# Unread products of the identity in TensorE's planned pauses, in a fused attention and recurrence kernel

## The chip, the cores and the metric

The kernel runs on one core of a Trainium2 chip. The metric is the device time of one execution in microseconds (us). The engines are TensorE (PE in the profile; its weight loads are PEld), VectorE (DVE), ScalarE (ACT), GpSimd (POOL) and SyncE (SP), which only issues transfers. "Granted clock" is the share of TensorE's full clock that its throttle lets through, as the profile records it.

## The reference, cut to what matters

Two layers follow each other on `x` of shape (16, 112, 512), all in float32. The first is a cross attention with 16 heads of width 32 over a normalised context of (16, 375, 512). The second is one block of a recurrent network: a data-dependent mix of each token with the one before it, five projections, a state of 16 x 16 per head (32 heads) that decays and takes in an outer product at each of the 112 steps, a normalisation over each head, a gate, and a feed-forward part.

```python
a = layer_norm(ctx)                         # attention
Q, K, V = x @ Wq.T, a @ Wk.T, a @ Wv.T      # per head
x = x + tanh(gate) * (softmax(Q K^T * scale) V) @ Wo.T

xa = ln(x); sx = shift(xa) - xa             # recurrence
xk, xw, xv, xr, xg = xa + sx * (maa + tanh-mix(xa, sx))
w = exp(-exp(time_decay + tanh(xw @ td_w1) @ td_w2))
def step(s, r, k, v, w):                    # 112 times
    return k v^T + w * s,  r . (u * k v^T + s)
x1 = x + group_norm(out) * silu(xg @ Wg.T) @ Wo.T
y = x1 + sigmoid(xr2 @ Wfr.T) * (relu(xk2 @ Wfk.T)**2 @ Wfv.T)
```

## The kernel before

**A recorder and a planner.** The program isn't written out in the order in which it runs. `planned` (line 599) calls the same operations on a `Recorder`, which only notes them. Generators for the parts (`attention`, and for each of eight groups of two batches `front`, `begin`, `middle` and `back`) note their operations with a place in an ideal order. A `Planner` (line 384) then plays through a model of the engines. Neighbouring TensorE products of one output are joined to a unit, every other operation is a unit of its own. `choose` takes the unit that can start first, with the place as a tie-break, and `commit` (line 532) books it: it gives each new tile a slot, asks a model of the array (`Array.run`, line 357) how long the products take, and notes when results and slots become free. `emit` (line 571) writes the instructions in exactly the planned order, with no reordering behind it, so that each engine's queue is the plan's order for that engine. The waits between engines come from the tiles that instructions share: who touches a tile waits for those before it in the plan's order that touched it in a way that conflicts.

**The model of TensorE.** For a full product of n columns `Array.run` counts `2 * (n * 2 / 2.4 + 2)` ns; for a transpose it takes the larger of a streaming term, `0.868` ns per column of the weights, and 109 ns. `Array.start` puts the start of a unit at the time when its inputs are ready or when the array is done, whichever is later. What lies between the array's end and that start is a pause in the plan. The plan knows nothing of the clock throttle.

**PSUM.** The eight banks of 512 float32 columns are seven slots of the tag `ps_bank`, which all products share in turn, and one of `ps_w`. `ps_w` holds the decays w of one chunk of channels: `decays_up` (line 1261) has VectorE clear its first columns and ScalarE write the rest with two exponentials, and `scans` (line 1301) has VectorE read it in two scans for each of the four steps of the chunk. It has 448 columns in use.

**The recurrence.** `middle` (line 1348) runs 16 steps n for each group. A step loads the values from DRAM, spread over partitions (`chk_kv`), multiplies them by the keys on VectorE and GpSimd, scans (VectorE, into `chk_st`, which has three slots), multiplies by r (GpSimd), and is summed by TensorE two steps later (`summed`, line 1321) with narrow products into one accumulator for each chunk. So a slot of `chk_st` is free again once TensorE has summed it. After the last step `back` follows: `norm_and_gate`, the projection `wo1`, a layer norm (its two sums are products with the constant `mean_w`), and the projections `wfk`, `wfr` and `wfv`.

**The tail.** Attention of later groups fills TensorE while a group's recurrence keeps VectorE and GpSimd busy. For the last two groups less and less of it is left.

## Time and profile before

| | us |
|---|---|
| median of 3 runs | 1387.72 (1385.05 to 1392.49) |
| the profiled execution, own time | 1388.27 |
| its span | 1386.5 |
| its mean granted TensorE clock | 0.963 |
| VectorE busy | 922.6 |
| GpSimd busy | 663.7 |
| ScalarE busy | 593.9 |

In the profile's rows an operation is named by its helper line (L596, the line of `emit` that calls all of them), so the names of the tiles tell groups apart: output tile, arrow, input tiles, with buffer numbers left out. A group's row has the number of instructions, the busy time and the mean duration of one, and then the idle time of the engine just before them with what ended it. A float32 product shows as two matmul records, each with a weight load of its own, and a transpose as one. The duration of a matmul record includes its way through the array; records overlap, so the pace of a row of products is read from the distance of their starts. A timeline row is start, duration of the merged piece, engine, operation, count, and in brackets the idle time before it. A row by stretches of time is the stretch, its length, busy time and records, the granted clock, and the share and rate of the DMA.

### The profile page before, as it was taken

How to read it: one execution, taken by the hardware profiler on the slowest of the kernel's cores; microseconds unless marked ns; L12 is line 12 of the kernel's file. 1: busy time of each engine (PE TensorE's matmuls, PEld its weight loads, DVE VectorE, ACT ScalarE, POOL GpSimd, SP SyncE). 2: the span in 40 equal slices, each digit the busy share in tenths (PEclk: the TensorE clock that was granted, in tenths of full speed). 3: DMA queues.
4: the chain of work that ended last, by engine and by line, in shares of the span. 5: the costliest groups of instructions: out<-in, count | busy, mean ns of one | idle time of the engine just before them, and what ended most of it. 6: DMA issues, size and time to landing. Idle time of an engine off the chain costs nothing.

```text
span 1386.5 us, 23595 instructions
## 1 busy us (share of the span) xinstructions
PE 1292.1 (93%) x8484; PEld 961.8 (69%) x8484; DVE 922.6 (67%) x1743; ACT 593.9 (43%) x1476; POOL 663.7 (48%) x644
## 2 busy tenths in 40 slices
PE   8999999989999999989999999989999898888867
PEld 5656577566966688566976589656985686767636
DVE  4345548975488664985577844994569669857942
ACT  2444624464245533664235631665325624233312
POOL 3001126843466442953546524771458357735750
PEclk9999999999999999999999999999999999979859
DMA  9401137321764057521774038521464155608621
GB/s 314 138 24 51 29 83 231 88 68 58 245 183 109 32 150 228 129 70 53 207 215 115 17 103 259 149 74 53 144 216 114 47 164 162 185 25 231 182 59 44
DMA packets 119990, 175.00 MB, mean 126 GB/s; under 512 B 14320, under 2 KB 92016, under 8 KB 119616
## 3 DMA queue, kind: packets, MB, share of 16 engines
q1 hardware_dynamic: 119232, 172.85, 42.9%
q8 instruction: 67, 1.10, 0.3%
q10 hardware_dynamic: 576, 0.52, 0.1%
q14 instruction: 51, 0.42, 0.1%
q0 software_dynamic: 64, 0.10, 0.0%
HBM read 164.52 MB, written 8.91 MB: 125 GB/s over the span
## 4 chain that ended last, share of the span: by engine, by line
PE 68%; DVE 13%; DMA 6%; ACT 5%; issue 4%; POOL 3%; SPq 1%; DVEq 0%; ACTq 0%; POOLq 0%
PE ps_bank L596 68%; DVE chk_st L596 5%; DMA chk_kv<-dram_vd 3%; ACT hp_pr L596 2%; DVE hp_pr L596 2%; DVE chk_kv L596 2%; POOL chk_st L596 1%; SPq L596 1%; DVE big_xa L596 1%; DMA ctxp_ctx<-in_ctx 1%; DMA slabs_slab<-in_wq 1%; ACT big_xa L596 1%; DMA slabs_slab<-in_wg 1%; ACT tmp_tmp L596 1%; DVE sm_st L596 0%
## 5 line engine op out<-in xcount | busy, mean ns | idle before, releaser
L596 POOL TENSOR_TENSOR chk_st<-chk_st,chk_r 128x448 f32<-128x448 f32 x256 | 316.2, 1257 | 137.1 <-DVE chk_st L596 133.5
L596 DVE TENSOR_TENSOR_SCAN chk_st<-ps_w_w,chk_kv 128x448 f32<-128x448 f32 x256 | 263.7, 1069 | 7.1 <-POOL chk_kv L596 4.6
L596 POOL TENSOR_TENSOR chk_kv<-chk_kv,chk_k 128x444 f32<-128x444 f32 x128 | 155.4, 1216 | 142.1 <-DMA chk_kv<-dram_vd 141.7
L596 PE MATMUL ps_bank<-big_x,slabs_slab 128*128 128x224 f32 x1024 | 205.0, 356 | 3.2 <-DMA slabs_slab<-in_wg 1.8
L596 PEld LDWEIGHTS ps_bank<-big_x,slabs_slab 128*128 128x128 f32 x1024 | 195.0, 192 | 10.6 <-issue 4.4
L596 PE MATMUL ps_bank<-ctxp_aT,keep_wk 128*128 128x375 f32 x512 | 174.2, 487 | 2.5 <-ACT hp_prT L596 2.0
L596 PE MATMUL ps_bank<-keep_wv,ctxp_aT 128*125 128x512 f32 x384 | 169.2, 592 | 0.0
L596 ACT ACTIVATE hp_pr<-hp_pr,sm_mn 112x375 f32<-112x375 f32 x256 | 152.9, 599 | 34.6 <-DVE sm_mn L596 34.1
L596 DVE TENSOR_TENSOR chk_kv<-chk_kv,chk_k 128x444 f32<-128x444 f32 x128 | 127.0, 995 | 45.9 <-DMA chk_kv<-dram_vd 45.7
L596 DVE CUSTOM_DVE_ANT_0 hp_pr<-ps_bank,hp_mb 112x375 f32<-112x375 f32 x256 | 124.8, 539 | 37.6 <-PE ps_bank L596 35.9
L596 PEld LDWEIGHTS ps_bank<-ctxp_aT,keep_wk 128*128 128x128 f32 x512 | 94.5, 191 | 65.2 <-ACT hp_prT L596 3.2
L596 PEld LDWEIGHTS ps_bank<-keep_wv,ctxp_aT 128*125 128x125 f32 x384 | 71.7, 188 | 84.0 <-issue 81.7
L596 PE MATMUL ps_bank<-chk_st,keep_td1c 128*32 128x224 f32 x1024 | 81.8, 375 | 33.2 <-POOL chk_st L596 28.5
L596 PE MATMUL ps_bank<-keep_ident,hp_pr 112*125 112x112 f32 x768 | 104.7, 281 | 8.6 <-ACT hp_prT L596 4.5
L596 PEld LDWEIGHTS ps_bank<-keep_ident,hp_pr 112*125 112x125 f32 x768 | 90.5, 188 | 31.4 <-ACT hp_prT L596 6.7
L596 POOL TENSOR_TENSOR big_x<-big_x,big_xa 128x448 f32<-128x448 f32 x48 | 59.8, 1260 | 82.2 <-DVE big_x L596 73.0
L596 ACT COPY chk_kv<-chk_s 128x8 f32<-128x8 f32 x112 | 22.5, 201 | 157.5 <-DMA chk_kv<-dram_vd 145.8
L596 PEld LDWEIGHTS ps_bank<-chk_st,keep_td1c 128*32 128x32 f32 x1024 | 29.7, 111 | 74.4 <-POOL chk_st L596 52.4
L596 DVE SCALAR_TENSOR_TENSOR big_x<-ps_bank,keep_vecs,big_sx 128x224 f32<-128x224 f32 x160 | 59.4, 440 | 26.7 <-PE ps_bank L596 26.6
L596 ACT COPY hp_prT<-ps_bank 125x448 f32<-125x448 f32 x112 | 58.2, 525 | 37.8 <-PE ps_bank L596 37.6
L596 ACT COPY kvp_v<-ps_bank 125x512 f32<-125x512 f32 x48 | 27.6, 582 | 99.0 <-PE ps_bank L596 99.0
L596 PE MATMUL ps_bank<-kvp_kT,kvp_qT 32*112 32x375 f32 x512 | 66.0, 519 | 0.2 <-ACT kvp_oR L596 0.2
(130 smaller groups left out, 1998.6 us busy)
## 6 DMA issues: line engine op xcount, KB each, us to landing
chk_kv<-dram_vd SPq DMA_DIRECT2D x512, 111.5 KB
slabs_slab<-in_wo SPq DMA_DIRECT2D x32, 512.0 KB
ctxp_ctx<-in_ctx SPq DMA_DIRECT2D x15, 672.0 KB
slabs_slab<-dram_wv1c SPq DMA_DIRECT2D x16, 512.0 KB
slabs_slab<-in_wk SPq DMA_DIRECT2D x16, 512.0 KB
slabs_slab<-in_wr SPq DMA_DIRECT2D x16, 512.0 KB
slabs_slab<-in_wg SPq DMA_DIRECT2D x16, 512.0 KB
slabs_slab<-in_wfk SPq DMA_DIRECT2D x16, 512.0 KB
```

Source lines behind the costliest of these rows:

```text
L596: call(*[real(a) for a in op.args], **{k: real(v) for k, v in op.kwargs.items()})
```

## The change

Wherever the plan has a pause of TensorE of more than 500 ns in front of a unit, and the unit's planned start lies after 30 us, the changed `emit` first issues products of the 128 x 128 identity with its own first 64 columns. Their number is 80% of (pause - 250 ns), divided by 110 ns and rounded down. Nobody reads the result. It goes to columns 448 to 511 of a bank: that of the unit itself, where the plan found its slot free before the array was done, and that of `ps_w` otherwise. For that the `ps_w` tile gets 512 columns, of which the first 448 are used as before. The planning isn't touched: the planned times don't count the new products, and all other instructions keep their order on every engine.

```diff
 SAME_MODE = 3.0
+PAUSE, FILL, FILLER, WARM, SPARE = 500.0, 0.8, 110.0, 30e3, 64
...
-        self.table = None
+        self.table, self.early = None, None
...
                 tile.slot = self.slot(tile)
+                if unit.engine == "tensor" and tile is unit.ops[0].writes[0].tile:
+                    unit.early = tile.slot.free_at <= self.array.end
...
         if engine == "tensor":
+            unit.pause = start - self.array.end if self.array.mode else 0.0
             ends = self.array.run(unit, start)
...
+    def spare(self, unit):
+        slot = unit.ops[0].writes[0].tile.slot if unit.early else None
+        slot = slot or self.recorder.tags["ps_w", "w"].slots[0]
+        return slot.real[:, 512 - SPARE : 512]
...
+        ident = self.recorder.tags["keep", "ident"].slots[0].real
...
+                if unit.engine == "tensor" and unit.pause > PAUSE and unit.start > WARM:
+                    spare = self.spare(unit)
+                    for _ in range(int((unit.pause - PAUSE / 2) * FILL / FILLER)):
+                        nc.tensor.matmul(spare, ident, ident[:, :SPARE], start=True, stop=True)
...
-            w_ps[c] = ps_w.tile([P, 2 * N], F32, tag="w", name=f"wp_{g}_{c}")
+            w_ps[c] = ps_w.tile([P, 512], F32, tag="w", name=f"wp_{g}_{c}")[:, : 2 * N]
```

In the changed program these are 610 products in 78 batches, the longest of 65. They raise TensorE's products from 4754 to 5364. 39 batches with 293 products write to the bank of `ps_w`, the others to a slot of `ps_bank`.

## The prediction

> **What bounds the kernel now.** I read the page's busy shares first, then the granted clock in its slices, then the chain that ended last.

> ```profile
> PE 1292.1 (93%) x8484; PEld 961.8 (69%) x8484; DVE 922.6 (67%) x1743; ACT 593.9 (43%) x1476; POOL 663.7 (48%) x644
> ```
> ```profile
> PEclk9999999999999999999999999999999999979859
> ```
> ```profile
> PE 68%; DVE 13%; DMA 6%; ACT 5%; issue 4%; POOL 3%; SPq 1%; DVEq 0%; ACTq 0%; POOLq 0%
> ```

> TensorE is busy 93% of the span and is 68% of the chain, so what delays it mostly delays the end. Its clock is full for most of 35 slices and drops in the last eight. The clock by stretches (us, PE busy and records, granted clock, DMA) shows all that there is to win:

> ```profile
> 297.68:301.09 3.41, 3.41 (x20) 0.50 0.85 225
> ...
> 1096.39:1103.22 6.83, 5.73 (x36) 0.50 0.00 0
> ...
> 1277.30:1290.96 13.66, 8.28 (x31) 0.50 0.38 90
> 1318.26:1348.99 30.73, 17.73 (x57) 0.50 0.16 44
> ...
> sum 102.43, PE 77.44; mean PE 5.96
> ```

> The thirteen throttled stretches last 102.4 us at clock 0.50, with 77.4 us of TensorE work in them. At full clock that work takes half, so the **gain is at most 38.7 us**: 6.7 before 1085 us, 9.0 from there to 1210, 6.8 in 1210 to 1240, 4.1 at 1277, 12.1 after 1310. Part of it is waiting for others and can't be won.

> **The price of one product.** The change adds 610 products in 78 batches, by the built program's order; nothing else moves on any engine, only waits are added. Every fp32 product is two records here, each with its own weight load (3730 products twice and 1024 transposes once make the 8484 of both rows); four products in a row with the same weights (mean_w of the late layer norms) still have eight loads, so an unchanged identity will be loaded again too. A pass streams 64 columns: 224 columns take 0.189 us in dense stretches (53 records in 10 us), so 0.054 us a pass and 0.108 a product, which is the planner's FILLER. But the weights are 128 columns wide. Two rows price their load (start, duration, what, count):

> ```profile
> 1313.46 0.30 PEld L596 LDWEIGHTS ps_bank<-tmp_tmp,keep_td1c 128*128 128x128 f32 x2 [0.82 <-ACT tmp_tmp L596]
> ```
> ```profile
> 332.42 1.39 PEld L596 LDWEIGHTS ps_bank<-keep_ident,hp_pr 112*125 112x125 f32 x12
> ```

> One load lasts 0.19 us, and two end after 0.30, so the second begins 0.11 after the first. Twelve transposes, whose matmuls stream less than the loads take, run at (1.39 - 0.19) / 11 = 0.109 us each. I take **0.109 us a pass, 0.218 a product**, twice what the planner thinks: 610 make 133 us. The ends are 0.108 (load hidden) and 2 x (0.19 + 0.054) = 0.49 (nothing overlaps); the value lies with the two rows that show loads back to back.

> [...]

> **Where the batches stand.** They fill 80% of a *planned* pause at half their real price; the trace has the real pauses. I laid each batch beside the gap of the trace in front of its product (start of that matmul less the end of streaming before it, less 0.15 us for the ordinary hand-over). "Excess" adds up what each batch takes beyond its own gap. "Carried" lets all idle time of TensorE in the stretch absorb lateness, and is what is left at its end.

> | us | batches, products | us at 0.218 | excess | carried |
> |---|---|---|---|---|
> | to 1085 | 47, 170 | 37.1 | 19.5 | 5.7 |
> | 1085 to 1200 | 9, 92 | 20.1 | 11.1 | 4.3 |
> | 1200 to 1240 | 8, 86 | 18.7 | 16.2 | 10.1 |
> | 1240 to 1310 | 4, 54 | 11.8 | 7.7 | 4.2 |
> | after 1310 | 10, 208 | 45.3 | 34.3 | 24.4 |

> In one ledger over the whole span the excess is 89 us and the carried lateness 46. 31 batches with 170 products stand before gaps under 0.2 us: the planner expected a pause that the chip doesn't have.

> A wait is added as well. 39 batches (293 products) write the last columns of the decay bank ps_w, which VectorE's scans read and ScalarE fills; they wait for the last such instruction before them in the plan's order, and later ones wait for them. Behind a waiting batch stand all of TensorE's products.

> **Stretch by stretch**, lateness against clock won:

> - To 1085 us: most of it is one long TensorE chain, with VectorE chains of 20 to 40 us between, where lateness is caught up. Midway between 5.7 and 19.5: +12. The eight-product batches in the 2.1 us pauses before 296, 614 and 935 fit, and lift windows like 294.27 to 297.68 (PE busy 1.55 us, then half clock) well above that. All 6.7 won: **+5.3**.
> - 1085 to 1200: batches of 10, 17, 27 and 12 overrun by 2.0, 2.6, 1.7 and 2.0; some is caught up behind DMA of chk_kv at 1174 to 1191. +7.6 less 6.5 of the 9.0: **+1.1**.
> - 1200 to 1240: 34 products wait for a VectorE memset of ps_w that ended at 1218.06, so end at 1225.5, and 1.3 us of summing and filling follows; the products of maa1 began at 1220.77. 31 more follow by 1230. The projection at 1234.44 starts some 7 us late, of which 3 come back by the full clock: **+4.0**.
> - 1240 to 1310: 26 products wait for the scan that ended at 1285.68, end at 1291.4, and the projection of 1288.38 becomes 3.4 late, less 1.2 of clock: **+2.2**.
> - After 1310: the decisive batch. Rows of TensorE, then of VectorE:

> ```profile
> 1322.99 3.14 PE L596 MATMUL ps_bank<-chk_st,keep_td1c 128*32 128x224 f32 x12 [3.26 <-POOL chk_st L596]
> 1326.63 0.96 PE L596 MATMUL ps_bank<-chk_st,keep_td1c 128*32 128x224 f32 x4 [0.50 <-POOL chk_st L596]
> ...
> 1335.09 0.96 PE L596 MATMUL ps_bank<-chk_st,keep_td1c 128*32 128x224 f32 x4 [0.29 <-POOL chk_st L596]
> ```
> ```profile
> 1332.73 1.09 DVE L596 TENSOR_TENSOR_SCAN chk_st<-ps_w_w,chk_kv 128x448 f32<-128x448 f32 x1 [2.39 <-POOL chk_kv L596]
> ```

>   Before the sums of chk_st that now run from 1325.17 on stand 65 products that wait for the *last* scan of the kernel, which ended at 1333.82. That scan is itself late: 12 products wait for the scan of 1316.74 and end at 1319.4, and the decays wait for them; 12 more end at 1324.2 and sums follow for 0.6; 32 then end at 1331.8, before the sum of 1322.99, which frees the slot of the last step's scan; that starts at 1332.6 in place of 1328.27. The last scan so ends at 1338.2, +4.3. Then 65 x 0.218 = 14.2 gives 1352.4, and 1.3 us of sums 1353.7, where they end at 1335.9 now: +17.8. In the closing chain the batches of 7, 31, 4, 15 and 29 add 0.5, 2.1, 0.6, 0.9 and 3.3, and the full clock takes 2.9 from the projection at 1343.27 and 3.1 from the two groups behind it: +1.4. Together **+19.2**.

> Sum: 5.3 + 1.1 + 4.0 + 2.2 + 19.2 = +31.8. The profiled execution took 1388.27 us (span 1386.5 and 1.8 around it), 0.6 over the median of 1387.72, so 1388.3 + 31.8 = **1420 us**, 2.3% slower.

> **What the clock needs** is the other open cost. In the trace a pass of 0.054 us streaming in 0.109 is 49% activity. A window at 331.81 with almost only transposes (45% streaming) kept the clock, and windows under 35% mostly lost it, so the fillers should hold it. At half clock a pass streams 0.107 us, beside 0.109 of load, so the price stays.

> [...]

> **Rivals.**

> 1. *The load of an unchanging weight is hidden* (faster). Then a product costs 0.108, the excess is 36 us and the carried lateness 2; about 12, less some 30 of clock: 1370 us. It decides below about 0.15 us a product, where lateness and gain balance. For it: a load can run beside a matmul. Against: loads never start closer than 0.11 in rows of two. Chance 0.12.
> 2. *Everything absorbs* (no change). The carried 46 less all 38.7: 1396 at most, a little under that where scans are ahead. For it: VectorE's full stretches at 240 to 290. Against: the closing chain has no slack. Chance 0.10.
> 3. *The clock isn't held*, since the identity's products don't count or TensorE stands idle at the new waits: +32 and about 30 not won, 1450; with the price over 0.3 more, over 1480. For it: 65 products wait some 5.7 us with TensorE idle. Chance 0.10.
> 4. The forecast, 1400 to 1457: chance 0.68. Its low end is the carried 46 less most of the clock, its high end the excess of 89 less half of it (1388 + 69).

> **Numbers.** About 0.5% (7 us) is what a measurement of this kernel can tell from no change. Faster 0.12 (rival 1), same 0.09 (most of rival 2), slower 0.79. The range 1393 to 1457 leaves out rival 1 and the upper half of rival 3.

> **What would show it.** In the profile after: 1220 added records of identity matmuls with a load each, starting 0.109 us apart; PEld busy up by over 100 us; the mean granted clock up from 0.963 to about 0.99; the 65 products as one block of 14 us right behind the last scan; new waits of VectorE and ScalarE on TensorE at ps_w; the long TensorE pieces before 1085 little changed. Loads closer than 0.08 us, or a block of 7 us, would make me wrong towards faster; a clock still at 0.5 in the closing 60 us towards slower.

## The result, and the profile after

The changed kernel takes **1460.34 us** (median of 4 runs, 1455.50 to 1462.31) against 1389.41 us (1385.05 to 1392.49) for the kernel before. The ratio is 1.0508, with a 95% interval of 1.0466 to 1.055. It is slower, as forecast, but by 71 us in place of 32, and 3 us above the range. The profiled execution has a span of 1460.3 us.

From the page of the kernel after, the busy shares, the granted clock in 40 slices, and the chain by engine:

```profile
PE 1415.4 (97%) x9704; PEld 1113.2 (76%) x9704; DVE 923.3 (63%) x1743; ACT 593.1 (41%) x1476; POOL 663.9 (45%) x644
```
```profile
PEclk9999999999999999999999999999999997988579
```
```profile
PE 78%; DVE 9%; DMA 5%; issue 3%; ACT 2%; POOL 2%; SPq 1%; DVEq 0%; ACTq 0%; POOLq 0%
```

The 1220 new records are there. VectorE, ScalarE and GpSimd are busy as long as before; only TensorE is busier, by 123 us, and its share of the chain rises from 68% to 78%. The clock row looks almost as it did: the mean granted clock is 0.965 against 0.963. The throttled stretches of the kernel after say more (stretch, length, PE busy and records, granted clock, DMA):

```profile
1200.38:1203.79 3.41, 3.41 (x10) 0.50 0.74 188
1220.86:1241.34 20.48, 20.32 (x96) 0.50 0.00 1
1289.13:1292.54 3.41, 3.41 (x9) 0.50 0.61 196
1306.19:1319.85 13.66, 13.66 (x61) 0.50 0.22 54
1347.15:1408.59 61.44, 54.35 (x277) 0.50 0.07 20
sum 102.40, PE 95.15; mean PE 19.03
```

Before 1200 us nothing is throttled any more (granted clock 1.00 from 30 to 1200 us, 0.99 in the kernel before): there the products do what the change is for. But the sum is 102.4 us again, as in the kernel before. The throttling has moved into the last 260 us, and in its longest stretches TensorE is busy most of the time (88% in the last one). It is busy mainly with the new products. Here is the last stretch, in TensorE's timeline after (start, duration, what, count, idle time before), in two pieces that meet at 1377 us:

```profile
1344.95 3.41 PE L608 MATMUL ps_w_w<-keep_ident 128*128 128x64 f32 x24 [2.31 <-DVE chk_st L611]
...
1350.55 5.35 PE L608 MATMUL ps_w_w<-keep_ident 128*128 128x64 f32 x24 [1.29 <-DVE chk_st L611]
1355.83 0.98 PE L611 MATMUL ps_bank<-chk_st,keep_td1c 128*32 128x224 f32 x8
1356.74 13.92 PE L608 MATMUL ps_bank<-keep_ident 128*128 128x64 f32 x64
1370.59 0.98 PE L611 MATMUL ps_bank<-chk_st,keep_td1c 128*32 128x224 f32 x8
```
```profile
1377.36 27.99 PE L608 MATMUL ps_w_w<-keep_ident 128*128 128x64 f32 x130 [5.80 <-DVE chk_st L611]
1405.29 2.47 PE L611 MATMUL ps_bank<-chk_st,keep_td1c 128*32 128x224 f32 x24
1407.69 2.19 PE L608 MATMUL ps_bank<-keep_ident 128*128 128x64 f32 x14
...
1410.52 7.03 PE L608 MATMUL ps_bank<-keep_ident 128*128 128x64 f32 x62
```

The 65 products (130 records, two to a product) stand behind the last scan, as forecast, and take 27.99 us, 0.215 a pass. The 32 products take 13.92 us, 0.218 a pass. At 1410.52 the clock is full again, and 62 records (31 products) take 7.03 us, 0.113 a pass. So a pass of these products took about twice as long at clock 0.50. VectorE's timeline after shows who waits for the two batches of 12 and 32 (the idle time is in the brackets):

```profile
1355.99 1.09 DVE L611 TENSOR_TENSOR_SCAN chk_st<-ps_w_w,chk_kv 128x448 f32<-128x448 f32 x1 [5.59 <-PE ps_w_w L608]
...
1371.76 2.07 DVE L611 TENSOR_TENSOR_SCAN chk_st<-ps_w_w,chk_kv 128x448 f32<-128x448 f32 x2 [8.63 <-PE ps_bank L611]
```

Both scans stand on the path to the last one. The first waits for the bank that the fillers write, the second for a slot of `chk_st` that the sum at 1370.59, behind the 32 products, sets free.

The same product's start after less its start before gives the lateness along the span (places by the kernel before): 3.7 us at 1197, 18.9 at 1238, 28 at 1311, 43.5 at the last scan (1332.73 before, 1376.22 after), 71.7 where the sums of chk_st end, 73.8 at the end. So 70 of the 74 us arise in the last fifth.

### The profile page after: what moved, and what is told of

Its sections match the earlier page's. It is cut to its first block, busy times and chain, and to the rows that moved or that the text cites. A ratio compares the mean times of both kernels' runs of the same rounds, so it can differ in the third digit from the quotient of the medians.

```text
span 1460.3 us, 26039 instructions
## 1 busy us (share of the span) xinstructions
PE 1415.4 (97%) x9704; PEld 1113.2 (76%) x9704; DVE 923.3 (63%) x1743; ACT 593.1 (41%) x1476; POOL 663.9 (45%) x644
## 4 chain that ended last, share of the span: by engine, by line
PE 78%; DVE 9%; DMA 5%; issue 3%; ACT 2%; POOL 2%; SPq 1%; DVEq 0%; ACTq 0%; POOLq 0%
PE ps_bank L611 67%; PE ps_w_w L608 6%; PE ps_bank L608 5%; DVE chk_st L611 4%; DMA chk_kv<-dram_vd 2%; DVE hp_pr L611 1%; SPq L611 1%; DVE chk_kv L611 1%; DMA ctxp_ctx<-in_ctx 1%; POOL chk_st L611 1%; DMA slabs_slab<-in_wq 1%; ACT hp_pr L611 1%; DMA dram_vd<-chk_v 1%; DMA slabs_slab<-in_wg 1%; ACT big_xa L611 0%
## 5 line engine op out<-in xcount | busy, mean ns | idle before, releaser
L611 DVE TENSOR_TENSOR_SCAN chk_st<-ps_w_w,chk_kv 128x448 f32<-128x448 f32 x256 | 264.1, 1071 | 27.6 <-PE ps_bank L611 8.6
L611 PE MATMUL ps_bank<-big_x,slabs_slab 128*128 128x224 f32 x1024 | 202.0, 353 | 1.7 <-DMA slabs_slab<-in_wg 1.7
L611 PEld LDWEIGHTS ps_bank<-keep_wv,ctxp_aT 128*125 128x125 f32 x384 | 71.7, 187 | 84.1 <-issue 81.0
L608 PE MATMUL ps_w_w<-keep_ident 128*128 128x64 f32 x586 | 100.3, 343 | 18.6 <-DVE chk_st L611 11.5
L608 PEld LDWEIGHTS ps_w_w<-keep_ident 128*128 128x128 f32 x586 | 95.6, 255 | 29.4 <-DVE chk_st L611 14.6
L608 PEld LDWEIGHTS ps_bank<-keep_ident 128*128 128x128 f32 x634 | 81.6, 208 | 8.5 <-issue 6.7
L608 PE MATMUL ps_bank<-keep_ident 128*128 128x64 f32 x634 | 84.9, 292 | 0.0
L611 PE MATMUL ps_bank<-chk_st,keep_td1c 128*32 128x224 f32 x1024 | 69.7, 374 | 3.9 <-DVE sm_mn L611 3.1
```

The source lines that it names most:

```text
L608: nc.tensor.matmul(spare, ident, ident[:, :SPARE], start=True, stop=True)
L611: call(*[real(a) for a in op.args], **{k: real(v) for k, v in op.kwargs.items()})
```

## The experiments

**Theory A** after this result: the long batches make the loss, since they run at half clock, where a pass costs 0.214 us because the weight load is slower too (333 ns in the block of 65, 192 ns in that at 1410.52), and where a stream that fills only half of the pass doesn't bring the clock back (27.99 us at 0.50 in the block of 65). As first put on record (e1), A also said that the clock falls because TensorE stands idle at the waits for the decay bank ps_w. **B**: every product costs about the same, wherever it stands. **C**: the waits at ps_w themselves cost the time. A further question came later: does the throttle look at the share of time in which columns stream (S), or does any work on the array satisfy it (L)? The kernels leave out or shorten only products that nobody reads. All in one table; the ratio is to the kernel before on the same chip:

| kernel | us | ratio (95%) |
|---|---|---|
| e1: own banks only, 317 products | 1404.31 | 1.0140 (1.0108 to 1.0171) |
| e4: e1, and one product at each place at ps_w, 356 | 1405.87 | 1.0140 (1.0089 to 1.0192) |
| e6: all but the six longest batches at ps_w, 444 | 1402.63 | 1.0115 (1.0072 to 1.0158) |
| e7: only those six, 166 | 1442.44 | 1.0397 (1.0359 to 1.0435) |
| e3: all 610, 64 weight columns | 1389.05 | 1.0028 (1.0009 to 1.0048) |
| e5: e1 with 64 weight columns | 1382.28 | 0.9968 (0.9950 to 0.9986) |
| e8: e6 with 64 weight columns | 1376.02 | 0.9915 (0.9884 to 0.9946) |
| e9: 64 weight columns, no batch over 12, 433 | 1381.87 | 0.9959 (0.9937 to 0.9980) |
| e10: e3 with 32 columns streamed | 1412.55 | 1.0179 (1.0139 to 1.0220) |
| e11: e8 with 32 columns streamed | 1378.97 | 0.9938 (0.9915 to 0.9962) |
| e12: e6 with 32 weight columns, 64 streamed | 1375.06 | 0.9904 (0.9881 to 0.9927) |

The kernel before had medians of 1387.43 (e1 to e5), 1387.81 (e6 to e9) and 1386.14 us (e10 to e12).

### e1: without the products at ps_w

```diff
-if unit.engine == "tensor" and unit.pause > PAUSE and unit.start > WARM:
+if unit.engine == "tensor" and unit.pause > PAUSE and unit.start > WARM and unit.early:
```

> Leaves out the 39 batches (293 products) that write the bank of ps_w; the 39 batches in the units' own banks (317 products) stay. Theory A (the loss is made at the waits for ps_w: TensorE stands idle there, the clock falls to 0.5, and the batch behind the wait then runs at 0.43 us a product): no wait is left, the products cost 0.218 us, their excess over the real pauses is some 10 to 48 us and most of the 38 us of throttling goes: 1385 to 1410 us, no idle time of TensorE that ScalarE's or VectorE's use of ps_w ends. Theory B (every product costs its load time, wherever it stands; the waits are incidental): 317 of 610 products keep about half of the +71 us: 1420 to 1430 us.

1404.31 us lies in A's range and below B's, but not for the reason that A gave here. No wait for ps_w is left, and A expected 0.218 us a product and most of the throttling gone. Yet the kernel is 17 us slower than before, its mean granted clock is 0.974, and its timeline of TensorE, with the clock of that stretch, shows that a batch needs no wait at ps_w to run at half clock and to stay there:

```profile
1318.78 13.92 PE L608 MATMUL ps_bank<-keep_ident 128*128 128x64 f32 x64
```
```profile
1318.78:1332.62 13.84, 13.84 (x66) 0.50 0.29 86
```

Narrow sums with pauses of 0.5 to 0.9 us go before it, the clock drops at 1317.5, before the batch, and 13.8 us of work without a gap don't lift it.

TensorE was busy for all of these 13.84 us at clock 0.50, so "busy" in the profile's sense was not enough to bring the full clock back.

### e4: the waits without the work

```diff
-for _ in range(int((unit.pause - PAUSE / 2) * FILL / FILLER)):
+for _ in range(int((unit.pause - PAUSE / 2) * FILL / FILLER) if unit.early else 1):
```

> Each of the batches in the bank of ps_w is cut to one product (39 or somewhat more in all, also where rounding gave none), so that every wait for ps_w stays; the batches in own banks are as in the changed kernel. Against the kernel without any product in ps_w (same call) this is the price of the waits alone. Theory A: the waits alone cost little, 5 to 15 us over that kernel, since they only become dear with a long batch behind them. Rival C: the waits cost most of the loss: 1430 us or more.

1405.87 us: 1.6 more than e1, which the two intervals don't tell from nothing (about 8 us either way), and less than the 5 to 15 that A allowed. The wait of the decisive place is still there, in TensorE's timeline of e4:

```profile
1339.18 0.69 PE L608 MATMUL ps_w_w<-keep_ident 128*128 128x64 f32 x2 [5.80 <-DVE chk_st L611]
1339.80 1.72 PE L611 MATMUL ps_bank<-chk_st,keep_td1c 128*32 128x224 f32 x16
```

The bracket says 5.80 us, as in the kernel after, but one product follows in place of 65. So the wait by itself isn't the cost, and C falls as a theory of the whole. The wait counts in that it sets where the batch starts, and in that TensorE is idle before it.

### e6 and e7: the six long batches at ps_w, out and alone

The batches of 17, 34, 26, 12, 12 and 65 products are left out (e6), or stand alone (e7).

```diff
-for _ in range(int((unit.pause - PAUSE / 2) * FILL / FILLER)):
+n = int((unit.pause - PAUSE / 2) * FILL / FILLER)
+n = 0 if n >= 12 and not unit.early else n
+for _ in range(n):
```

(e7 has `n = n if n >= 12 and not unit.early else 0`.)

> The changed kernel without six batches: those of 17, 34, 26, 12, 12 and 65 products that write the bank of ps_w (166 products). The other 444 products and their waits stay, all with 128 columns of weights. Theory A (the loss is made by long batches that begin behind a wait for ps_w at half clock): the greater part of the loss goes, 1398 to 1415 us. Theory B (each product costs about 71 / 610 = 0.12 us): 166 x 0.12 = 19 us go, 1440 us.

> Only those six batches, 166 products, all others left out. Theory A: 1425 to 1445 us, with a batch of 65 that lasts some 27 us at clock 0.50. Theory B: 1389 + 19 = 1408 us.

Without the six: 1402.63 us, 15 more than before. Only the six: 1442.44 us, 55 more. Both lie in A's ranges, and far from the 1440 and 1408 of B. The two add up to 69 of the 71 us of the whole change, so 27% of the products carry three quarters of the loss. In e7 no block of 32 goes before the 65, and they are as slow (TensorE's timeline of e7):

```profile
1357.89 27.99 PE L610 MATMUL ps_w_w<-keep_ident 128*128 128x64 f32 x130 [9.25 <-DVE chk_st L613]
```

### e3: half the weight columns

```diff
-nc.tensor.matmul(spare, ident, ident[:, :SPARE], start=True, stop=True)
+nc.tensor.matmul(spare[:SPARE], ident[:, :SPARE], ident[:, :SPARE], start=True, stop=True)
```

> All 610 products at their places and with all their waits, but each with 64 columns of weights instead of 128 (it writes 64 partitions). If the load of 128 columns sets the pace (0.109 us a pass at full clock, 0.214 at half), a pass now takes about 0.055 us, a product 0.11 and the array streams nearly all the time, so that a batch that begins at half clock brings the full clock back within some 3.4 to 7 us. Theory A: 1385 to 1405 us, the batch of 65 lasts 7 to 11 us in place of 27.6. Rival C (the waits for ps_w themselves are the loss, whatever the batch does): 1430 us or more. If the pace isn't set by the load: no change, 1455 to 1462.

1389.05 us: the same 610 products at the same places, with the same waits, cost 71 us less, so C, which said 1430 or more, falls here too. The block of 65 in TensorE's timeline of e3, and its clock in windows:

```profile
1330.48 9.51 PE L608 MATMUL ps_w_w<-keep_ident 128*64 128x64 f32 x130 [8.04 <-DVE chk_st L611]
```
```profile
1330.90:1334.30 3.40, 3.40 (x35) 0.50 0.00 0
1334.30:1341.00 6.70, 6.70 (x121) 1.00 0.01 2
```

It starts at half clock after 8.04 us of idleness, and from 1334.30, 3.82 us after its start, the clock is full. Two things changed at once, though: the load has half the columns, and a pass takes 0.062 us at full clock (58 in 3.60 us at 1359.66) in place of 0.113, so that the same 64 columns, an estimated 0.054 us, fill most of it. e10 parts them.

### e10 and e11: half the stream as well

```diff
-nc.tensor.matmul(spare[:SPARE], ident[:, :SPARE], ident[:, :SPARE], start=True, stop=True)
+nc.tensor.matmul(spare[:SPARE, :32], ident[:, :SPARE], ident[:, :32], start=True, stop=True)
```

> All 610 products with 64 weight columns as in the run that came to 1389.05, but 32 columns streamed in place of 64: a pass is then a load of 64 columns (about 0.055 us at full clock, 0.109 at half) beside a stream of half its length. Theory S (the throttle looks at the share of time in which columns stream): the price at full clock stays, but the block of 65 behind the last scan no longer brings the clock back, so lasts about 14 us in place of 9.3, and the blocks of 32 and 31 can slow down too; 1395 to 1415. Theory L (the throttle is satisfied by any work of the array, and only loads of all 128 columns failed to bring the clock back): block of 65 about 8 to 9.5 us, time 1385 to 1391.

> The same products of 64 weight columns and 32 streamed columns, without the six long batches that wait at ps_w (444 products); the same with 64 streamed columns took 1376.02. Theory S: the blocks of 32 and 31 near the end run at half clock (7 us each in place of 4.7 and 3.6), the clock is held less, 1380 to 1395. Theory L: 1374 to 1379.

e10 takes 1412.55 us: half as many columns are streamed, and it is some 21 to 24 us slower than e3 (by the ratios and by the medians). Its timeline of TensorE, and the clock over three blocks of it:

```profile
1335.26 7.04 PE L608 MATMUL ps_bank<-keep_ident 128*64 128x32 f32 x64
...
1349.00 14.07 PE L608 MATMUL ps_w_w<-keep_ident 128*64 128x32 f32 x130 [5.80 <-DVE chk_st L611]
...
1386.74 1.94 PE L608 MATMUL ps_bank<-keep_ident 128*64 128x32 f32 x30
```
```profile
1335.26:1342.23 6.97, 6.97 (x69) 0.50 0.17 36
1349.00:1363.00 14.00, 14.00 (x130) 0.50 0.00 1
1386.74:1388.68 1.94, 1.94 (x31) 1.00 0.35 141
```

At full clock a pass costs what it cost in e3 (15 products take 1.94 us, against 1.96), so the load is the same. At half clock it costs 0.108, and the block of 65 stays there for its whole 14 us, as S expected. With loads of 64 columns in both, the block of 65 was at full clock 3.82 us after its start with 64 columns streamed (e3), and at 0.50 for 14.00 us with 32 (e10). In e11 the blocks of 32 and 31 run at half clock too (7.04 and 6.82 us against 4.89 and 3.83 in e8), as S said. But the total of 1378.97 lies 1 us below S's range and inside L's, and its interval overlaps that of e8: here S is right by its blocks and missed by its time. That the 5 us of slower blocks are hidden where scans end later is not shown.

### e5, e8, e9, e12: a version that is faster

These change which batches stand and how wide the weights are; their edits are those of e1, e6 and e3 together, `n = min(n, 12)` with e3's weights for e9, and `spare[:32], ident[:, :32], ident[:, :SPARE]` for e12.

> Only the batches in own banks, with 64 columns of weights: 317 products of 0.11 us, 35 us in all, no waits for ps_w. Theory A: excess 1 to 19 us against up to 30 us of clock: 1365 to 1390 us, the only one of the four that can beat the kernel before; the clock after 1310 us is at half for less than 15 us. Theory B: near 1400 us.

> As the kernel with 64 columns of weights, but without the six batches: 444 products of 0.11 to 0.12 us, short waits for ps_w only. With half weights the sums of chk_st around the batch of 65 came 6 to 15 us later than in the kernel before, and were 2 us early just before it. Theory A: that goes, 1376 to 1385 us, below the kernel before. If the six batches were what brought the clock back: 1388 us or more, with long stretches at 0.50 after 1275 us.

> 64 columns of weights, and no batch longer than 12 products (1.4 us at full clock), at all 78 places and with all waits: 433 products. Theory A: the waits for the last scans stay, so that TensorE stands idle there and the clock falls for some 14 us at the end, but nothing long follows a wait: 1376 to 1390 us. If the idle time at the waits were itself dear, it would stay with the kernel with half weights, 1387 to 1392.

> 32 weight columns and 64 streamed columns, without the six long batches (444 products): the load is then shorter than the stream, so a pass is bound by 64 columns of streaming, 0.054 us in place of 0.059 to 0.062. Both theories: the clock is held as with 64 weight columns, and the time is that of that kernel (1376.02) or up to 4 us less; 1371 to 1378.

All four lie in the ranges expected and, by their intervals, below the kernel before. e8 (1376.02) and e12 (1375.06) win most, 0.85% and 0.96% on the kernel before. Two rows of e8's TensorE, the blocks that took 13.92 and 13.33 us with 128 weight columns in e6:

```profile
1313.82 4.89 PE L610 MATMUL ps_bank<-keep_ident 128*64 128x64 f32 x64
...
1333.60 3.83 PE L610 MATMUL ps_bank<-keep_ident 128*64 128x64 f32 x62
```

With the same 444 products, 128 weight columns cost 15 us against the kernel before and 64 win 12. Capping all batches at 12 (e9) wins less than dropping the six, though the two intervals still touch. A likely reason, not tested alone, is that its last short batch at ps_w waits with TensorE idle for 9.63 us and runs slowly (24 records in 2.82 us at 1333.93, against 1.61 us at 1341.23). 32 weight columns (e12) are no clear gain over 64: the 29 products near the end take 3.43 us in place of 3.60, so halving the load again shortens a pass only from 0.062 to 0.059 us.

## Why the prediction was right in sign and wrong in size

**Right: the price at full clock.** 0.109 us a pass was forecast from two rows of loads; a batch of 31 took 7.03 us for 62 passes, 0.113 each, and its records start 0.111 to 0.112 apart.

**Right: the part before 1200 us.** All throttling there is gone (clock 1.00 from 30 to 1200 us), and the lateness is 3.7 us where 6.4 was summed (5.3 and 1.1). The products that fit their pauses do hold the clock, and most lateness is caught up. That the sum came so close is partly luck: it took the middle between two bounds (5.7 and 19.5 us up to 1085, whose middle is 12.6 and not 12), and no run tests that choice. The prediction also misread the clock row before: the digits below 9 stand in the last five slices, not in the last eight.

**Right: the decisive place.** The block of 65 stands behind the last scan, and the sums behind the block. The closing chain behind those added 2.1 us (71.7 to 73.8) where 1.4 was forecast.

**Wrong: one step, "At half clock a pass streams 0.107 us, beside 0.109 of load, so the price stays".** It took the load's duration as independent of the clock. The load slows with it, so a pass takes 0.214 and a product 0.43. The trace of the kernel before already showed this. Its loads of 128 columns between 1343.3 and 1348.9 us, at clock 0.50, and between 1351 and 1355 us, at full clock, are these groups (count, then busy time and mean ns of one):

```profile
L596 PEld LDWEIGHTS ps_bank<-big_o,slabs_slab 128*128 128x128 f32 x16 | 5.2, 334 | 3.9 <-POOL big_o L596 3.4
```
```profile
L596 PEld LDWEIGHTS ps_bank<-xp_x,keep_td1c 128*128 128x128 f32 x8 | 1.4, 189 | 0.3 <-DVE xp_x L596 0.3
```

The fillers' own loads last the same: 333 ns in the block of 65 and 192 ns in that at 1410.52. A load that kept its 0.109 us and merely stopped overlapping with 0.107 us of streaming would also make 0.214 a pass, but then a pass of e3 would take about 0.16 at half clock, and it took 0.107: its 3.40 us at 0.50 are touched by 35 records, where 0.16 would leave room for some 24.

The step before it, "the fillers should hold the clock", is wrong for the same stretch: I drew 49% streaming as enough from windows that began at full clock, and both that share and the 45% of the window at 331.81 are estimates. Blocks that began at full clock mostly kept it, as at 1410.52 (7.03 us) and up to 1200 us (clock 1.00); blocks that began at 0.50 stayed there, in e1 for 13.8 us, in the block of 65 for 28 us and in e10 for 14 us. The batches behind waits at ps_w and behind thin sums are those that start at half clock, or lose the full clock soon after their start (the 26 at 1304.84 after 1.35 us, the first 12 at 1344.95 after 2.2).

What this step is worth, batch by batch. The two longest batches before 1310 us, in TensorE's timeline after:

```profile
1221.02 14.77 PE L608 MATMUL ps_w_w<-keep_ident 128*128 128x64 f32 x68 [4.31 <-DVE ps_w_w L611]
```
```profile
1304.84 10.15 PE L608 MATMUL ps_w_w<-keep_ident 128*128 128x64 f32 x52 [1.27 <-DVE chk_st L611]
```

The times of seven batches (us):

| products | forecast at 0.218 | measured |
|---|---|---|
| 34, at 1221.02 | 7.4 | 14.77 |
| 26, at 1304.84 | 5.7 | 10.15 |
| 12, at 1344.95 | 2.6 | 3.41 |
| 12, at 1350.55 | 2.6 | 5.35 |
| 32, at 1356.74 | 7.0 | 13.92 |
| 65, at 1377.36 | 14.2 | 27.99 |
| 7, at 1407.69 | 1.5 | 2.19 |
| sum | 41.0 | 77.8 |

That is 36.8 us too little, all in batches that hold up every TensorE product queued behind them. The span missed by 73.8 - 31.8 = 42.0. By stretches the misses fit: 11 us from 1200 to 1240 (15.2 in place of 4.0, 7.4 of it the batch of 34), 7 from there to 1311 (9.1 in place of 2.2, 4.5 of it the batch of 26), 27 after (46 in place of 19.2, 24.9 of it the last five), less 2.7 before 1200. The other 8 us of these stretches I haven't traced one by one; one part is the projection at 1315.82, which was to run at full clock and ran at half for its first 4 us.

**The rivals.** A hidden load and full absorption fell with the price. The third, "the clock isn't held", with a chance of 0.10 and 1450 us, or more where the price rises too, is what happened in the last fifth of the span. It named two conditions. The first, that the identity's products don't count, is half true: at 0.50 they didn't bring the clock back in 28 us with 128 weight columns, and they did 3.82 us after their start with 64 (e3). The second, TensorE idle at the new waits, costs little by itself (1.6 us in e4), but the block of 65 behind such a wait starts at half clock (clock 0.50 up to 1334.30 in e3). One of the signs that the prediction named for "slower" is there: the clock is at 0.50 until 1408.59, in the closing 60 us.

## What to carry to other kernels

To keep TensorE's clock with dummy products, make their weights no wider than what they stream: with 64 or 32 weight columns for 64 streamed, the same 444 products turned from 15 us of loss into 11 to 12 of gain. Price such a product at half clock too (0.43 us here, 0.22 at full clock), since it may run there, and leave it out where it must wait for a buffer that an engine on the path still reads: here the 65 products behind the last scan delayed the sums behind them by their full 28 us. Busy time of TensorE doesn't tell its clock (13.84 us fully busy at 0.50 in e1); read the granted clock over the block itself.

## What the runs showed of the hardware

Products of a kind that ran on at full clock did not bring it back from 0.50. By an estimate from 224 columns in 0.189 us, the fillers with 128 weight columns stream in 0.054 of the 0.112 us of a pass. The kernel after ran 62 of their records in 7.03 us at 1410.52, at clock 1.00. At 0.50 the same records stayed at 0.50 to the end of the block, over 13.84 us in e1, and over 13.85 and 27.93 us in the kernel after. The block of 65 with 64 weight columns was at full clock 3.82 us after its start with 64 columns streamed (e3), and at 0.50 for 14.00 us with 32 (e10).

No run was made to find the least streaming that holds the clock or brings it back.

The weight loads took longer with more columns and at a lower granted clock. In the kernel before, loads of 125x32 (`hp_prT`) took 109 ns in the mean, and loads of 128x128 189 ns at full clock and 334 ns at 0.50. Where the fillers stand back to back, a pass with 128 columns of weights started every 0.112 us at full clock and every 0.213 at half (kernel after), and one with 64 columns of weights and 32 streamed every 0.058 and 0.107 (e10: 58 records in 3.57 us, and 130 in 14.07).
